# First batch's rows loaded and normalised ahead of the context, and two exponentials moved by one product

## The chip, the cores and the metric

The kernel runs on one core of one Trainium2 chip. The metric is the device time of one execution in microseconds (us). A core has five engines, each with its own instruction queue: PE (TensorE, matrix products), DVE (VectorE, elementwise work and reductions), ACT (ScalarE, functions and copies), POOL (GpSimd, elementwise work beside DVE) and SP (SyncE, which issues most of the loads and stores). ACT can issue loads too. Engines wait for each other through semaphores.

## The reference, cut to what matters

Two decoder layers over x, of two batches, 512 rows of 1024 columns each, with a context of 1024 rows of 1024 columns per batch. All is float32.

```python
x = x + L0_xattn(layernorm(x), ctx)   # fake_quant(x1) @ fake_quant(ctx)
x = x + L0_ffn(layernorm(x))          # linear, plus a mixture of low-rank terms
x = x + L1_xattn(layernorm(x), ctx, ctx, mask)   # 32 heads, 8 key/value heads, rotary
x = x + L1_ffn(layernorm(x))          # linear, plus one low-rank expert per row

def layernorm(x):
    return (x - mean(x)) / sqrt(var(x) + 1e-5)
def fake_quant(x, s, z):
    return (clip(round(x / s + z), 0, 255) - z) * s
```

Layer 0's attention is a plain product of the quantized, normalised rows with the quantized context. Layer 1's keys and values depend on the context alone, so they need nothing of layer 0.

## The kernel before, in words

**Products.** Large float32 products go block by block through a form with seven block products in place of eight (`seven`, `seven_onto`). The seven products need sums and differences of the input blocks (`left_steps`, L233 to L241, for the weights; `right_steps`, L247 to L255, for the context), and the results are put together again by additions on DVE (L278, L281, L283, L287, L290). The products stand on PE in the order 1, 2, 6, 7, 5, 4, 3, and each adds up in a PSUM bank; there are four such banks (tag `b`), so a product can also wait for DVE or ACT to have read an older bank. One product is four matrix multiplications of 128 by 512, shown in the profile as eight matmuls (L345), about 3.43 us.

**The first stage.** The keys of the first batch come first, while the weights and the context arrive. `first` holds four chains of products: two heads of quad 0 (`first[0]`) and two of quad 1 (`first[1]`). Their products 1 and 2 use raw blocks and need nothing of DVE. Product 6 of the first head is the first that needs DVE: L250 and L236. A finished key block is rotated (`rope_steps`, two ACT copies L204 and L205, then L207, L210 and L211 on DVE) and written away (`kT`, L487). This stage is written inside a block in which DVE and ACT keep the program's order; the PE order is as written in the whole kernel. All the other instructions are placed by a scheduler, which may also put later work between those of the block. So where an instruction stands on its engine is read from the built program, not from the source.

**Loads.** SP issues the weights, the context and the rotary tables, then a list of small constants: the four quantization scales and zero points (L1066), router and gate constants (L1067 to L1070). The rows of the first batch (`load_rows(0, nc.scalar)`) are issued by ACT, behind the first stage.

**Layer 0 beside the keys.** `layer_0` is a chain of side steps. `weave` advances it by one step after every second product of the main work, which is the rest of `first[1]` (ten products), then the values, and so on. For a batch, `quantized_product` loads eight context row blocks, quantizes each in three DVE operations (L182, L185, L186) into `q2`, then takes four row blocks: statistics (two L151 and one L152), square root on ACT (L163), reciprocal (L164), scaling (L156), quantizing (L182, L185, L186). Two steps behind, `turned` transposes a row block on PE (L424), copies it out and forms its row sum on ACT (L427). Then come the column sums (L447) and the product (L461) with its additions.

**Start of attention.** The last queries' products are worked off in the first turns of `attention` (`extra["products"]`). For each head the scores (L763) go to two wide PSUM tiles and are added to the mask on DVE (L777); a tree of maxima follows (L785 to L791), which PE transposes (L727, also into a wide tile) and DVE reduces (L729). `place_maximum` copies the maximum to PSUM on ACT (L805), and `exponential(j)` adds it on DVE (L809) and takes the exponential on ACT (L812). In the turn before the first head is attended to, four query products are done, numbered by `i`; before, the first exponential follows product `i == 1` and the second `i == 2`.

Of the kernel before, what the change touches and what calls it, by code (L numbers as in the profile page):

```python
# [13 lines left out]
BF16 = mybir.dt.bfloat16  # L14
# [25 lines left out]
def decoder_kernel(  # L40
# [38 lines left out]
    def u8(shape, dtype=F32):  # L79
        return new(shape, "u8", 14, dtype)  # L80

    def u4(shape, dtype=F32):
        return new(shape, "u4", 17, dtype)
# [56 lines left out]
    def copy_out(dst, src):  # L140

        evac[0] += 1
        if evac[0] % 2:
            nc.scalar.copy(dst, src)
        else:
            nc.vector.tensor_copy(dst, src)
# [12 lines left out]
    def layernorm(x_t):  # L159
        mv = small([P, 2])  # L160
        moments(x_t, mv)
        rstd = small([P, 1])
        nc.scalar.activation(rstd, mv[:, 1:2], AF.Sqrt, bias=eps_t)  # L163
        nc.vector.reciprocal(rstd, rstd)  # L164
        return scaled(x_t, mv[:, 0:1], rstd)
# [14 lines left out]
    def quantized(dst, src, side):  # L180

        nc.vector.tensor_scalar(  # L182
            src, src, qp[f"{side}_inv"], qp[f"{side}_zp"], ALU.mult, ALU.add
        )
        nc.vector.tensor_scalar(src, src, 0.0, QMAX, ALU.max, ALU.min)  # L185
        nc.vector.tensor_scalar(dst, src, RND, RND + QMID, ALU.add, ALU.subtract)  # L186
# [185 lines left out]
    def rows(b, t):  # L372
        return x[b][t // 2][:, t % 2, :]
# [33 lines left out]
        return right_sums(nc.vector, *quarters, lambda: u8([P, 4, HALF]))  # L407


    def quantized_product(b):  # L410
        q2 = [u8([P, 4, D], BF16) for _ in range(2)]
        for k in range(NKT):
            c_t = u4([P, D])
            nc.sync.dma_start(c_t, ctx_in[b, ts(k, P), :])
            quantized(q2[k // 4][:, k % 4, :], c_t, "x2")
            if k % 2:
                yield
        x1T = u8([P, NC, S], BF16)
        rsum, l1s = [], []

        def turned(t):
            tr = ps_wide().bitcast(BF16)[:, 0 : NC * P].rearrange("p (c n) -> p c n", c=NC)
            for c in range(NC):
                nc.tensor.transpose(tr[:, c, :], l1s[t][:, ts(c, P)], ident_b)  # L424
            copy_out(x1T[:, :, ts(t, P)], tr)
            r = small([P, 1])
            nc.scalar.activation(u4([P, D]), l1s[t], AF.Copy, accum_out=r)  # L427
            nc.vector.tensor_scalar(r, r, c_x2, None, ALU.mult)
            rsum.append(r)

        for t in range(NT):
            h = layernorm(rows(b, t))
            l1 = u2([P, D], BF16)
            quantized(l1, h, "x1")
            l1s.append(l1)
            if t > 1:
                turned(t - 2)
            yield
        turned(NT - 2)
        yield  # L440
        turned(NT - 1)


        cs = ps_wide()
        for n in range(2):
            for k in range(NKT):
                nc.tensor.matmul(  # L447
                    cs[:, ts(n, HALF)],
                    ones_b,
                    q2[k // 4][:, k % 4, ts(n, HALF)],  # L450
                    start=(k == 0),
                    stop=(k == NKT - 1),
                )
        csum = u4([P, D])
        nc.vector.tensor_scalar(csum, cs, kc2, c_x1, ALU.add, ALU.mult)
        yield
        for t in range(NT):
            acc = ps_wide()
            for n in range(2):
                for c in range(NC):  # L460
                    nc.tensor.matmul(  # L461
                        acc[:, ts(n, HALF)],
                        x1T[:, c, ts(t, P)],
                        q2[c // 4][:, c % 4, ts(n, HALF)],
                        start=(c == 0),
                        stop=(c == NC - 1),
                    )
            y = u4([P, D])
            nc.vector.scalar_tensor_tensor(y, acc, rsum[t], csum, ALU.add, ALU.add)
            xs = rows(b, t)  # L470
            nc.vector.scalar_tensor_tensor(xs, y, s12, xs, ALU.mult, ALU.add)
            yield
# [378 lines left out]
    def attention(extra):  # L851

        total = B * NH
        heads, outs, kv = {}, {}, {}
        stretches = iter(())

        def rotate():  # L860
            for rotation in extra["later"]:
                next(rotation, None)
            extra["later"].clear()

        def begin(n):
            if n >= total:
                return
            gg = n // GRP
            if gg not in kv:
                b, g = gg // NKV, gg % NKV  # L870
                kT = u4([P, S2])
                nc.sync.dma_start(kT, kT_d[b][g])
                v = u4([P, NKT, DH])
                nc.sync.dma_start(v, v_d[b][g // 2][:, :, ts(g % 2, DH)])
                kv[gg] = kT, v
                outs[gg] = u8([P, GRP, S])
            heads[n] = Head(n, kv[gg], outs[gg][:, n % GRP, :])

        begin(0)
        for n in range(-2, total + GRP + 1):  # L880
            new, mid, old = heads.get(n + 2), heads.get(n + 1), heads.get(n)
            begin(n + 3)
            if new:
                for j in range(4):
                    new.scores(j)
            yield

            if n - 1 in heads:
                heads.pop(n - 1).normalize()
            if n == GRP - 1 or n == NH:  # L890
                fetch_rows(n // NH)

            if GRP <= n <= total and n % GRP == 0:
                oT = outs.pop(n // GRP - 1)
                sums = u8([P, 3, 2, 256])
                places = iter(range(3))
                o_ops = left_sums(
                    nc.gpsimd,
                    oT[:, 0:2, 0:256],
                    oT[:, 2:4, 0:256],  # L900
                    oT[:, 0:2, 256:S],
                    oT[:, 2:4, 256:S],
                    lambda: sums[:, next(places)],
                )
                following = n // GRP - 1, o_ops
            tree = new.tree() if new else iter(())
            k = (n - 1) % GRP
            if n > GRP and k == 0:
                gg, o_ops = following
                stretches = projection(gg // NKV, o_ops, dict(w_ops))  # L910
            for _ in range(3 + k % 2 if n > GRP else 0):
                next(stretches, None)
                next(tree, None)
            if n > GRP and gg + 1 < B * NKV:
                for i in {2: (1, 6, 2), 3: (7, 5, 4, 3)}.get(k, ()):
                    w_ops[i] = output_operand((gg + 1) % NKV, i)
            for i in range(extra.pop(n, 0)):
                for _ in range(2):
                    next(tree, None)
                next(extra["products"])  # L920

                if mid and not old and i == 1:
                    mid.place_maximum()
                    mid.exponential(0)
                if mid and not old and i == 2:
                    mid.exponential(1)
            if n == GRP:
                w_ops = {i: output_operand(0, i) for i in (1, 6, 2, 7, 5, 4, 3)}
            for _ in tree:
                pass  # L930
            yield

            if mid and old:
                mid.place_maximum()
            if old:
                old.turn_sum()
            elif new:
                new.turn_maximum()
            rotate()
            if old:  # L940
                old.attend(0)
                if mid:
                    mid.exponential(0)
                if new:
                    new.turn_maximum()
                if mid:
                    mid.exponential(1)
                old.den = from_row(old.den)
            if new:
                new.nmx = from_row(new.nmx)  # L950
            if old:
                old.attend(1)
            yield
# [114 lines left out]
    nc.sync.dma_start(eb_t, ebias.partition_broadcast(P))  # L1068
    nc.sync.dma_start(r0_t, r0T.rearrange("(c p) e -> p c e", p=P))
    nc.sync.dma_start(ga_t, gaT.rearrange("(c p) e -> p c e", p=P))  # L1070


    ctx_ops = [ctx_raw[0], ctx_raw[2]] + [None] * 5
# [5 lines left out]
    first = [keys(0, 0, ctx_ops, w[0], begun), keys(0, 1, ctx_ops, w[1])]  # L1079

    def layer_0():
        yield from quantized_product(0)
        put_away(0)
        x[1] = halves()
        load_rows(1, nc.sync)
        yield from quantized_product(1)

    with tc.manual_schedule(engines={mybir.EngineType.DVE, mybir.EngineType.Activation}):
# [25 lines left out]
        for i, _ in enumerate(chain(*first[0])):  # L1114
            if i in (4, 5, 6, 7):
                w[1][:] = next(lefts) or w[1]

        x[0] = halves()
        load_rows(0, nc.scalar)

    for side in ("x1", "x2"):
        nc.vector.reciprocal(qp[f"{side}_inv"], qp[f"{side}_scale"])
# [309 lines left out]
```

## Time and profile before

| what | us |
|---|---|
| median of 4 runs | 2437.22 |
| lowest and highest run | 2435.51 and 2437.6 |
| the profiled execution | 2435.51 |
| its span, first to last instruction | 2433.7 |
| PE busy | 2405.6 |
| DVE busy | 1841.5 |
| POOL busy | 1025.1 |
| ACT busy | 527.5 |

The granted clock of PE is 0.999 of full speed over the span. The page gives busy times by engine, a strip of the span in forty slices, the transfers, the chain of work that ended last and the costliest groups of instructions. A group's row names the source line, the engine, the operation, the tile written and those read, the shape, the count, then busy time, the mean of one in ns, and the idle time of the engine before them with what ended it. The waits' rows give the total, the number and the longest. Rows in order of time begin with the start and the length, and end with the idle time before them in brackets. Buffer numbers are left out of names.

### The profile page before, as it was taken

What the parts mean: (1) busy time and instruction counts of PE and PEld (TensorE: products, weight loads), DVE (VectorE), ACT (ScalarE), POOL (GpSimd) and SP (SyncE); (2) the same over time, 40 slices, a digit from 0 to 9 for tenths busy, and PEclk for the clock granted to TensorE, in tenths of its full rate; (3) what the DMA queues carried; (4) which work ended last, traced back from release to release, by engine and by line L of the source; (5) the groups of instructions that cost most, each with busy time, mean ns of one, the idle gap of its engine ahead of it and who ended that gap; (6) DMA issues with size and microseconds to landing.
All of it is one profiled execution on the core that took longest, in us unless ns stands there. A gap on an engine that the chain in (4) does not pass through costs nothing.

```text
span 2433.7 us, 19521 instructions
## 1 busy us (share of the span) xinstructions
PE 2405.6 (99%) x6784; PEld 1194.2 (49%) x6792; DVE 1841.5 (76%) x1998; ACT 527.5 (22%) x623; POOL 1025.1 (42%) x543
## 2 busy tenths in 40 slices
PE   9999999999999999999999999999999999999999
PEld 4477458654444444444444444444444444444444
DVE  5849774345886556898888888888898988888753
ACT  1210221011222222322222222222223222222210
POOL 0000010210000001777676767667776767677531
PEclk9999999999999999999999999999999999999999
DMA  5437233013796221344234423542442344233501
GB/s 197 169 102 278 70 134 109 26 61 116 271 331 223 78 87 55 95 149 116 68 86 108 117 66 91 143 140 76 135 117 78 92 126 116 67 91 109 173 9 61
DMA packets 151506, 288.01 MB, mean 118 GB/s; under 512 B 32112, under 2 KB 49776, under 8 KB 149104
## 3 DMA queue, kind: packets, MB, share of 16 engines
q1 hardware_dynamic: 110880, 244.54, 31.6%
q10 hardware_dynamic: 40384, 41.70, 5.9%
q8 instruction: 54, 0.88, 0.2%
q0 software_dynamic: 144, 0.52, 0.1%
q14 instruction: 44, 0.36, 0.1%
HBM read 223.54 MB, written 63.18 MB: 118 GB/s over the span
## 4 chain that ended last, share of the span: by engine, by line
PE 55%; DVE 4%; issue 1%; POOL 0%; ACT 0%; POOLq 0%; ACTq 0%; DVEq 0%
PE b L345 20%; PE wide L763 16%; PE b L826 16%; PE wide L727 2%; DVE u L809 1%; DVE u L789 0%; DVE u L787 0%; DVE small L729 0%; DVE u L777 0%; DVE u L318 0%; PE b L967 0%; PE wide L192 0%; DVE u L791 0%; POOL u L818 0%; POOL u L819 0%
## 5 line engine op out<-in xcount | busy, mean ns | idle before, releaser
L345 PE MATMUL b<-u,u 128*128 128x512 f32 (+1 forms) x3600 | 1383.4, 541 | 17.0 <-DVE u L283 5.5
L345 PEld LDWEIGHTS b<-u,u 128*128 128x128 f32 x3600 | 680.4, 190 | 686.0 <-issue 603.5
L826 PE MATMUL b<-u,u 128*128 128x512 f32 x1024 | 460.3, 593 | 0.0
L763 PE MATMUL wide<-u,u 128*128 128x512 f32 x1024 | 452.4, 593 | 2.5 <-DVE u L777 1.8
L815 POOL TENSOR_TENSOR u<-u 128x1024 f32<-128x1024 f32 x64 | 151.6, 2368 | 707.0 <-ACT u L812 698.4
L777 DVE TENSOR_TENSOR u<-wide,u 128x1024 f32<-128x1024 f32 x256 | 312.7, 1223 | 126.1 <-PE wide L763 125.8
L812 ACT ACTIVATE u<-u 128x2048 f32<-128x2048 f32 x128 | 244.7, 1911 | 655.7 <-DVE u L809 651.3
L763 PEld LDWEIGHTS wide<-u,u 128*128 128x128 f32 x1024 | 192.9, 190 | 250.7 <-issue 175.6
L809 DVE TENSOR_TENSOR u<-u,b 128x2048 f32<-128x2048 f32 x128 | 290.1, 2267 | 3.0 <-ACT b L805 3.0
L826 PEld LDWEIGHTS b<-u,u 128*128 128x128 f32 x1024 | 186.2, 192 | 184.6 <-issue 184.6
L300 POOL TENSOR_TENSOR u<-u,u 128x512 f32<-128x512 f32 x120 | 184.4, 1563 | 170.3 <-DVE u L312 134.6
L318 DVE TENSOR_TENSOR u<-u,b 128x512 f32<-128x512 f32 x200 | 135.7, 679 | 121.7 <-PE b L345 114.3
L818 POOL TENSOR_TENSOR u<-u,u 128x1024 f32<-128x1024 f32 x64 | 150.7, 2354 | 30.6 <-ACT u L812 30.2
L819 POOL TENSOR_TENSOR u<-u,u 128x1024 f32<-128x1024 f32 x64 | 150.7, 2355 | 5.0
L837 POOL TENSOR_TENSOR u<-u,u 128x512 f32<-128x512 f32 x64 | 116.8, 1826 | 18.9 <-DMA u<-row 18.8
L204 ACT ACTIVATE u<-u 64x512 f32<-64x512 f32 x72 | 45.2, 628 | 361.9 <-DVE u L283 166.3
L785 DVE TENSOR_TENSOR u<-u 128x1024 f32<-128x1024 f32 x64 | 111.6, 1744 | 0.0
L727 PEld LDWEIGHTS wide<-ident,u 128*128 128x128 f32 x512 | 80.0, 203 | 62.2 <-issue 56.2
L605 POOL TENSOR_TENSOR u<-u,u 128x1024 f32<-128x1024 f32 x8 | 20.2, 2529 | 213.1 <-DVE u L156 210.5
L787 DVE TENSOR_TENSOR u<-u,u 128x1024 f32<-128x1024 f32 x64 | 106.5, 1664 | 0.2
L820 POOL TENSOR_TENSOR u<-u 128x512 f32<-128x512 f32 x64 | 100.1, 1563 | 5.0
L1158 POOL DMA_DIRECT2D u<-in_b_dram x1 | 0.7, 717 | 228.4 <-PE b L345 228.4
(136 smaller groups left out, 1638.5 us busy)
## 6 DMA issues: line engine op xcount, KB each, us to landing
u<-row ACTq DMA_DIRECT2D x128, 256.0 KB, 3.7
u<-wo SPq DMA_DIRECT2D x64, 512.0 KB, 4.6
u<-in_wo_dram SPq DMA_DIRECT2D x48, 512.0 KB, 4.6
u<-in_wq_dram SPq DMA_DIRECT2D x32, 512.0 KB, 4.3
q<-u SPq DMA_DIRECT2D x64, 256.0 KB, 2.3
u<-in_wo_dram SPq DMA_DIRECT2D x16, 1024.0 KB, 7.7
wo<-u SPq DMA_DIRECT2D x32, 512.0 KB, 3.5
u<-q SPq DMA_DIRECT2D x64, 256.0 KB, 4.5
```

Source lines behind the costliest of these rows:

```text
L300: nc.gpsimd.tensor_tensor(c, c, what, ALU.add)
L318: nc.vector.tensor_tensor(c, c, acc, ALU.add)
L345: nc.tensor.matmul(acc, lhsT, rhs, start=start and k == 0, stop=k == len(pairs) - 1, skip_group_check=True,)
L727: nc.tensor.transpose(tr[:, t, :], src[:, t, :], ident)
L763: nc.tensor.matmul(sc[:, ts(n, HALF)], self.kT[:, ts(2 * j + n, P)], self.qT, start=True, stop=True,)
L777: nc.vector.tensor_tensor(self.e[j // 2][:, js, :], sc.rearrange("p (k q) -> p k q", k=2), mask[j], ALU.add)
L809: nc.vector.tensor_tensor(e, e, self.nmf.unsqueeze(1).to_broadcast([P, 4, S]), ALU.add)
L812: nc.scalar.activation(e, e, AF.Exp)
L815: nc.gpsimd.tensor_tensor(d, e[:, 0:2, :], e[:, 2:4, :], ALU.add)
L818: nc.gpsimd.tensor_tensor(d, d, e[:, 0:2, :], ALU.add)
L819: nc.gpsimd.tensor_tensor(d, d, e[:, 2:4, :], ALU.add)
L826: nc.tensor.matmul(self.acc, self.v[:, k, :], self.e[j][:, k % 4, :], start=(k == 0), stop=(k == NKT - 1),)
```

## The change

The rows of batch 0 are issued by SP, directly behind the constants, instead of by ACT behind the first stage. For batch 0 alone `quantized_product` takes the rows ahead of the context. There the statistics of all four row blocks come first, one square root and one reciprocal serve all four, and then each block is scaled and quantized as before. The order for batch 1 stays: context, then rows, a root for each. In `attention` both exponentials of the first head are called one product later.

```diff
-    def quantized_product(b):
-        q2 = [u8([P, 4, D], BF16) for _ in range(2)]
-        for k in range(NKT):
-            c_t = u4([P, D])
-            nc.sync.dma_start(c_t, ctx_in[b, ts(k, P), :])
-            quantized(q2[k // 4][:, k % 4, :], c_t, "x2")
-            if k % 2:
-                yield
-        x1T = u8([P, NC, S], BF16)
-        rsum, l1s = [], []
+    def quantized_product(b, rows_first=False):
+        q2, x1T, rsum, l1s = [], [], [], []
+
+        def quantized_context():
+            q2.extend(u8([P, 4, D], BF16) for _ in range(2))
+            for k in range(NKT):
+                c_t = u4([P, D])
+                nc.sync.dma_start(c_t, ctx_in[b, ts(k, P), :])
+                quantized(q2[k // 4][:, k % 4, :], c_t, "x2")
+                if k % 2:
+                    yield
...
-        for t in range(NT):
-            h = layernorm(rows(b, t))
-            l1 = u2([P, D], BF16)
-            quantized(l1, h, "x1")
-            l1s.append(l1)
-            if t > 1:
-                turned(t - 2)
-            yield
-        turned(NT - 2)
-        yield
-        turned(NT - 1)
+        def quantized_rows():
+            x1T.append(u8([P, NC, S], BF16))
+            mv, rstd = small([P, NT, 2]), small([P, NT])
+            if rows_first:
+                for t in range(NT):
+                    moments(rows(b, t), mv[:, t, :])
+                nc.scalar.activation(rstd, mv[:, :, 1], AF.Sqrt, bias=eps_t)
+                nc.vector.reciprocal(rstd, rstd)
+            for t in range(NT):
+                if rows_first:
+                    h = scaled(rows(b, t), mv[:, t, 0:1], rstd[:, t : t + 1])
+                else:
+                    h = layernorm(rows(b, t))
+                l1 = u2([P, D], BF16)
+                quantized(l1, h, "x1")
+                l1s.append(l1)
+                if t > 1:
+                    turned(t - 2)
+                yield
+            turned(NT - 2)
+            yield
+            turned(NT - 1)
+
+        parts = [quantized_context, quantized_rows]
+        for part in reversed(parts) if rows_first else parts:
+            yield from part()
...
                 if mid and not old and i == 1:
                     mid.place_maximum()
-                    mid.exponential(0)
-                if mid and not old and i == 2:
-                    mid.exponential(1)
+                if mid and not old and i > 1:
+                    mid.exponential(i - 2)
...
     nc.sync.dma_start(ga_t, gaT.rearrange("(c p) e -> p c e", p=P))
+    x[0] = halves()
+    load_rows(0, nc.sync)
...
     def layer_0():
-        yield from quantized_product(0)
+        yield from quantized_product(0, True)
...
-        x[0] = halves()
-        load_rows(0, nc.scalar)
```

More of the change, by code (lines that the diff above doesn't have):

```diff
@@ L424, in turned @@
                 nc.tensor.transpose(tr[:, c, :], l1s[t][:, ts(c, P)], ident_b)
-            copy_out(x1T[:, :, ts(t, P)], tr)
+            copy_out(x1T[0][:, :, ts(t, P)], tr)
             r = small([P, 1])
@@ L462, in quantized_product @@
                         acc[:, ts(n, HALF)],
-                        x1T[:, c, ts(t, P)],
+                        x1T[0][:, c, ts(t, P)],
                         q2[c // 4][:, c % 4, ts(n, HALF)],
```

## The prediction

> **What bounds the kernel now.** I read the page's busy shares first, then the waits of PE (TensorE), then the time-ordered rows of DVE (VectorE) where those waits lie.
>
> ```profile
> PE 2405.6 (99%) x6784; PEld 1194.2 (49%) x6792; DVE 1841.5 (76%) x1998; ACT 527.5 (22%) x623; POOL 1025.1 (42%) x543
> ...
> L345 PE MATMUL b<-u,u 128*128 128x512 f32 (+1 forms) x3600 | 1383.4, 541 | 17.0 <-DVE u L283 5.5
> ```
>
> PE is busy for 2405.6 of 2433.7 us, so an edit pays only by the PE idle time that it removes or makes. In the first 400 us the waits of PE are:
>
> ```profile
> PE b L345 <- DVE u L283: 4.2, 2, 3.4
> PE b L345 <- ACT u L274: 4.1, 1, 4.1
> PE b L345 <- DVE u L281: 3.9, 3, 1.6
> ```
>
> Behind the first stand these DVE rows (start, length, idle before in brackets):
>
> ```profile
> 77.79 0.69 DVE L151 BATCH_NORM_STATS2 small<-u 128x6 f32<-128x512 f32 x1 [2.39 <-DMA u<-in_x_in_dram]
> ...
> 84.78 0.81 DVE L182 TENSOR_SCALAR u<-u,qp_x_inv,qp_x_zp 128x1024 f32<-128x1024 f32 x1 [1.74 <-DMA u<-in_ctx_in_dram]
> 85.51 0.68 DVE L283 TENSOR_TENSOR u<-u,b 128x512 f32<-128x512 f32 x1
> ```
>
> DVE works in order: while L182 waits for a context row, L283, which PE needs, stands behind it, and PE idles 82.83 to 86.25. The ACT wait of 4.12 (121.92 to 126.04) is the same on the scalar engine: copy L274 stands behind square root L163, which waits for a row's statistics. Between lie waits of 1.27 and 0.75; together 9.56. Two stretches also ran at half clock (length, busy, ..., PEclk, DMA):
>
> ```profile
> 85.80:89.20 3.40, 2.95 (x4) 1.40 (x5) 3.40 (x6) 1.26 (x2) 0.00 (x0) 0.50 1.03 413
> 126.75:130.17 3.42, 3.42 (x9) 2.68 (x9) 3.28 (x6) 0.77 (x2) 0.00 (x0) 0.50 1.04 375
> ```
>
> Half of the PE time in them is lost: (89.21 - 86.25)/2 = 1.48 and 3.42/2 = 1.71, so 3.2. What the stage after 45 us loses is 9.56 + 3.2 = 12.8.
>
> **Part 1, what is saved.** Rows go first: their statistics, one root and four scalings are done before the context rows are wanted, and quantizing the context (eight rows of 0.72 + 0.60 + 0.60 = 1.93 by L182, L185, L186, 15.4 in all) moves into the first value products, where DVE owes PE one 0.6 operation per 3.43 us product. So all four waits can go. The new order still has four rows' scaling and quantizing, 4 x (0.72 + 1.93) = 10.6, in the key products; one late L281 there may leave about 0.6 (estimate; ends 0, and 3.4 as the longest such wait before). Saved: 12.8 - 0.6 = 12.2. The four row loads leave ACT's queue (0.33 to 0.46 each), which is not the bound; on SP they stand ahead of the first kT write, which nobody waits for in this stage. The context loads now stand behind kT writes on SP; before they landed 4.0 to 10.6 us after issue. Quantizing starts with the value products, near 118 (111 before, plus some 7 that Part 2 costs by then beyond what is saved), takes 15.4, and shares DVE with the last key rotations (some 6): done near 140. The column sums of L447, which need all eight rows, are due near 150, so the cover is some 10 us.
>
> **Part 2, what it costs.** The built order of the changed kernel shows what the diff does not. On DVE the six small operations on the quantization constants (L1122 to L1126 before) now stand ahead of the first difference L247, and a BN_STATS of row 0 stands between L247 and L250. Before:
>
> ```profile
> 20.13 2.29 DVE L247 TENSOR_TENSOR u<-u,u 128x2048 f32<-128x2048 f32 x1 [18.20 <-DMA u<-in_ctxT_in_dram]
> 24.10 2.29 DVE L250 TENSOR_TENSOR u<-u,u 128x2048 f32<-128x2048 f32 x1 [1.68 <-DMA u<-in_ctxT_in_dram]
> 26.31 1.22 DVE L233 TENSOR_TENSOR u<-u,u 128x1024 f32<-128x1024 f32 x1
> 27.56 1.22 DVE L236 TENSOR_TENSOR u<-u,u 128x1024 f32<-128x1024 f32 x1
> 28.70 0.68 DVE L207 SCALAR_TENSOR_TENSOR u<-b,cos_t 128x512 f32<-128x512 f32 x1
> ```
>
> The constants' loads are issued at 17.3 to 24.0 and land 10.8 to 4.6 us later, all near 28.1 to 28.6. So L247 starts at 29.1 instead of 20.13. Steps from start to start: 2.20 for 2048 columns, 1.14 for 1024, 0.60 for 512 or a BN_STATS, 0.12 for an aggregate. L247 ends its step at 31.3. Row 0 is issued behind the last constant (27.97 + 0.4 = 28.4). A load of the same 512 KB on a quiet SP queue (in_wv) took 4.0 to 4.8; I take 4.0, so 32.4. Below it is ga_t's 2.7 (144 KB, the load just ahead), above it 5.7, the first x row before, which shared the queues with context loads. Then:
> - BN 0.6, L250 2.2, L233 1.14, BN 0.6, L236 1.14, L207 0.68 to its end: 38.8. Product 6 of the first head needs them and the PSUM bank that L207 frees; PE comes to it at 12.56 + 6 x 3.43 = 33.1. PE waits 5.7.
> - L207, L210, aggregate, BN, L211, L252, L238, L207 to its end: 38.1 + 0.6 + 0.6 + 0.1 + 0.6 + 0.6 + 2.2 + 1.1 + 0.7 = 44.7, product 7. It runs to 48.1.
> - L210, BN, L211, L241, L255, aggregate, three BN, aggregate, L207 from 44.5: 0.6 + 0.6 + 0.6 + 1.1 + 2.2 + 0.1 + 1.8 + 0.1 + 0.7 = 52.4: product 5 waits 4.3 for the next bank.
> - L210, BN, L211, aggregate, L207, L210 to 55.4; reciprocal behind the one root on ACT (table load 1.28 + 0.30 after the aggregate at 54.3, 55.9; behind the root on ACT stands L204, which waits for L283 until 58.8 anyway); L211, L278 with its 0.78 step, L281 to its end: 58.1, product 4.
>
> Product 4 started at 44.74 before (after a wait of 0.94): 13.4 later. DVE sets this time all along, so PE's clock in it hardly counts. Part 1 and 2: 13.4 - 12.2 = +1.2.
>
> The trace went to half clock after the waits of 3.42 and 4.12, for 3.41 us each, from 85.79 and 126.75; in the 3.41 us before these points PE had still worked 0.45 and 0.71 us. The Trainium skill (TensorE: Matmul & The Clock Gate, Part 1) has a free-running window of about 3.4 us and a drop after at least one idle window. By its letter neither wait here should have brought the drop, and of the new ones only the 5.7 one must. The sum is the same by both: with a full clock product 5 would end 1.4 earlier and product 4 still wait for L281 until 58.1.
>
> The same page (Architectural detail) calls ACT and DVE strict FIFO. This rule speaks against the change, and the rows at 77.79 to 85.51 bear it out. Were it not so, L247 could pass the waiting constants, and the time would be that of the first rival below.
>
> **Part 3, exponentials a product later.** Before (PE, then DVE, at the start of attention):
>
> ```profile
> 959.29 3.70 PE L345 MATMUL b<-u,u 128*128 128x512 f32 x8 [1.25 <-DVE u L278]
> ```
>
> ```profile
> 956.35 2.29 DVE L809 TENSOR_TENSOR u<-u,b 128x2048 f32<-128x2048 f32 x1 [2.98 <-ACT b L805]
> 958.56 0.68 DVE L278 TENSOR_TENSOR u<-u,b 128x512 f32<-128x512 f32 x1
> 959.15 2.28 DVE L809 TENSOR_TENSOR u<-u,b 128x2048 f32<-128x2048 f32 x1
> 963.03 0.69 DVE L281 TENSOR_TENSOR u<-u,b 128x512 f32<-128x512 f32 x1 [1.60 <-PE b L345]
> 963.64 0.68 DVE L729 TENSOR_REDUCE small<-wide 128x4 f32<-128x512 f32 x1
> ```
>
> In the new order L278 comes before the first L809 and L281 before the second. L278 then starts when its product ends, 958.08 instead of 958.56: saved 0.5. But the second L809 (2.20) now stands between L281 (962.55) and the reduction L729: 962.55 + 0.6 + 2.2 = 965.35, ending at 966.05. L729 frees the PSUM tile of the second score pair of L763, which PE wants at 962.8 + 1.7 = 964.5: a new wait of 1.5. The third pair wants the tile that the first L777 frees at 965.35 + 3 x 0.6 + 1.2 = 968.4, and PE is there at 967.85: 0.55, and some 0.1 for restarting. Net +1.7. The rest of the shift is covered: the second exponential on ACT (L812, 1.91, begun at 961.47 before) ends near 967.5 instead of 963.4, and its first reader, attend (L826), starts at 977.6; the row of the next maximum is issued on ACT behind it (L736, 964.35 before), 3 us later, lands near 973 and is copied by L805 at 981. Ends: -1.25 if both new waits are covered, +2.2 if the old wait stays.
>
> **Sum.** +1.2 + 1.7 = +2.9. The profiled execution took 2435.5 (span 2433.7 and 1.8 around it), the lowest of the four runs; the median is 2437.2, so the times would be 2438.4 and 2440.1. I say 2440.
>
> **Rivals.**
> - Faster: the constants land early enough not to hold DVE. For it: they are 0.5 KB each. Against: landings of 4.6 to 10.8 us behind the weights. Without the 9 us the stage costs eight BN_STATS and four aggregates (5.3) instead of 13.4, total -5.2: 2432. It decides if L247 starts by about 21. Chance 0.08.
> - Slower: row 0 lands late, as the x rows did before (5.7, 8.1, 9.6, 11.2). Each us past 4.0 moves product 4 by one us; past 6.0 the whole is over 0.2% slower. At 8.1: +7.0, 2444. For it: the rows follow ten loads on one queue. Against: the queues are nearly empty at 28 us. Chance 0.24.
> - DVE stays short in the key products, since it also carries 10.6 us of row work; waits like the old 3.42 return. Price +3 to +4: 2443. Against: no row waits for a load there. Chance 0.16.
>
> **How the numbers follow.** The forecast has 0.52. Its own ends are -1.3 and +1.7 (row 0), +-1.5 (where the clock's steps fall) and -3.0 to +0.5 (part 3), roughly 2436 to 2443. Leaving out the faster rival and half of the slow one gives 2434.5 to 2445. Within 0.2% (4.9 us, about what a measurement of this kernel can tell from no change) lie most of the forecast and half of the third rival: 0.54. Slower: 0.39. Faster: 0.07.
>
> **What would show it.** DVE idle until about 28.6, then L247, then about 1 us waiting for in_x; PE waits on L345 of some 5.7 and 4.3 between 33 and 53; none over 1 from 60 to 150; L763 waiting for L729 near 964. It is wrong if L247 still starts near 20, if row 0 lands beyond 6 us, or if waits of 2 us or more remain in the key products.

## Result and the profile after

The changed kernel takes 2441.12 us (median of 35 runs, 2438.0 to 2444.0) where the kernel before takes 2437.55 (median of 55). The ratio is 1.0015, with a 95% interval of 1.0011 to 1.0020: 3.6 us slower, and clearly so, though by less than 0.2%. Forecast were 2440.0 and +2.9. The profiled execution took 2442.7 (span 2440.9), 7.2 more than the profiled one of before; the pair of profiles exaggerates the change, for a reason that comes below.

PE stays the bound. The page's first part and its largest group, of the changed kernel:

```profile
PE 2408.7 (99%) x6784; PEld 1194.3 (49%) x6792; DVE 1839.7 (75%) x1995; ACT 527.3 (22%) x620; POOL 1025.5 (42%) x543
...
L345 PE MATMUL b<-u,u 128*128 128x512 f32 (+1 forms) x3600 | 1386.1, 542 | 18.6 <-DVE u L207 9.4
```

The matmuls of L345 are idle ahead for 18.6 us instead of 17.0, and the main releaser is another one: the rotation L207 (keys), no longer the sums L281 and L283. The waits of PE in the first 400 us (total, times, longest) say where:

```profile
PE b L345 <- DVE u L207: 9.4, 2, 5.8
PE b L345 <- DVE u L281: 2.3, 2, 1.7
```

The waits of 3.42, 1.27, 0.75 and 4.12 us in the kernel before are gone, and two of 5.78 and 3.65 have come. DVE's rows, in order of time, show how they come about:

```profile
28.00 0.16 DVE L1136 RECIPROCAL qp_x_inv<-qp_x_scale 128x1 f32<-128x1 f32 x1 [26.08 <-DMA qp_x_scale<-in_x_scale_dram]
...
28.77 2.28 DVE L247 TENSOR_TENSOR u<-u,u 128x2048 f32<-128x2048 f32 x1
32.95 0.69 DVE L151 BATCH_NORM_STATS2 small<-u 128x6 f32<-128x512 f32 x1 [1.90 <-DMA u<-in_x_in_dram]
33.56 2.27 DVE L250 TENSOR_TENSOR u<-u,u 128x2048 f32<-128x2048 f32 x1
...
59.32 0.69 DVE L283 TENSOR_TENSOR u<-u,b 128x512 f32<-128x512 f32 x1 [0.81 <-PE b L345]
```

DVE stands idle for 26.08 us, until a constant of 0.5 KB lands at 28; L247, which ran at 20.13 before, starts at 28.77; then DVE waits 1.90 us for row 0 before it may start L250 (24.10 before). L283 runs at 59.32, against 44.79 before. What PE made of it, in its own rows (start, length, instructions, and the idle time before):

```profile
39.35 9.81 PE L345 MATMUL b<-u,u 128*128 128x512 f32 x16 [5.78 <-DVE u L207]
52.81 9.47 PE L345 MATMUL b<-u,u 128*128 128x512 f32 x15 [3.65 <-DVE u L207]
...
344.64 5.85 PE L345 MATMUL b<-u,u 128*128 128x512 f32 x13 [1.70 <-DVE u L281]
...
963.21 3.70 PE L345 MATMUL b<-u,u 128*128 128x512 f32 x8 [0.85 <-DVE u L278]
...
970.49 1.98 PE L779 MATMUL wide<-u,u 128*128 128x512 f32 x4 [1.39 <-DVE small L745]
972.82 3.70 PE L779 MATMUL wide<-u,u 128*128 128x512 f32 x8 [0.34 <-DVE u L793]
...
995.28 3.70 PE L779 MATMUL wide<-u,u 128*128 128x512 f32 x8 [0.65 <-DVE u L793]
```

(Lines of attention stand 16 lower than before: scores L763 are now L779, the reduction L729 is L745, the additions of the mask L777 are L793.) The wait for L278 is 0.85 instead of 1.25, and three new waits follow, for the reduction and twice for an addition of the mask behind it.

The row at 344.64 is a useful mark. The same product, with much the same wait ahead of it, stands in the profile before:

```profile
343.18 7.13 PE L345 MATMUL b<-u,u 128*128 128x512 f32 x16 [1.65 <-DVE u L281]
```

Everything that parts 1 and 2 of the change touch lies ahead of it, part 3 far behind it. So it splits one profile into three stretches: to this mark (parts 1 and 2), from it to the product that waits for L278 near 959 (no part of the change), and from there to the transposes that wait for L791 (L807 after) near 1043 (part 3). The table below has all runs of this study, the differences of medians taken against the kernel before in the same series, the stretches from each kernel's one profile:

| kernel | against before, us | 95% interval of the ratio | mark near 343, against 343.18 | mark to L278's product | from there to L791's transposes |
|---|---|---|---|---|---|
| before | | | 0 | 616.1 | 84.1 |
| changed | +3.6 | 1.0011 to 1.0020 | +1.5 | 618.6 | 86.8 |
| exponentials undone | +1.2 | 0.9997 to 1.0015 | +2.1 | 617.1 | 83.6 |
| exponentials alone | +2.6 | 1.0005 to 1.0022 | +0.4 | 615.9 | 86.8 |
| constants early | +4.0 | 1.0007 to 1.0025 | +3.2 | 614.7 | 86.8 |
| rows by hand | +1.6 | 0.9996 to 1.0014 | +1.2 | 612.8 | 86.8 |
| rows and constants by hand | -3.5 | 0.9974 to 0.9991 | -6.7 | 618.4 | 86.8 |
| statistics between, exponentials undone | -11.1 | 0.9937 to 0.9962 | -12.3 | 618.4 | 83.6 |
| statistics between | -8.1 | 0.9945 to 0.9972 | -12.5 | 621.6 | 86.8 |
| rows late | +4.7 | 1.0006 to 1.0024 | +1.3 | 615.9 | 86.8 |

The middle stretch runs from 612.8 to 621.6 us though no kernel changes anything in it: in all ten profiles each engine's instructions, from 2 us behind the mark to 6 us ahead of L278's product, are the same and in the same order. It is as long as its waits make it. PE's waits of more than 0.25 us there add up to 1.36 us in the shortest and 8.42 in the longest; waits of up to 2 us between 600 and 760 come and go (one of 2.04 at 664.70 in the changed kernel's profile). That is how two single profiles can be 7.2 us apart where the medians are 3.6 apart. What makes these waits come and go stays open, and it need not be chance alone: constants early and rows by hand, which have the shortest middle stretches, are by their medians 1.9 and 2.3 us faster than their other two stretches add up to, and the two kernels with the statistics between 1.7 slower. So a median prices an edit only to some 2 us, and the stretch that holds the edit is the better measure.

### The profile page after: what moved, and what is told of

Its sections match the earlier page's. It is cut to its first block, busy times and chain, and to the rows that moved or that the text cites. A ratio compares the mean times of both kernels' runs of the same rounds, so it can differ in the third digit from the quotient of the medians.

```text
span 2440.9 us, 19522 instructions
## 1 busy us (share of the span) xinstructions
PE 2408.7 (99%) x6784; PEld 1194.3 (49%) x6792; DVE 1839.7 (75%) x1995; ACT 527.3 (22%) x620; POOL 1025.5 (42%) x543
## 4 chain that ended last, share of the span: by engine, by line
PE 84%; DVE 9%; DMA 3%; issue 2%; POOL 1%; ACT 1%; SPq 0%; POOLq 0%; DVEq 0%; ACTq 0%
PE b L345 47%; PE wide L779 16%; PE b L842 15%; PE wide L743 2%; DVE u L825 2%; DMA u<-in_wo_dram 1%; PE wide L477 1%; PE wide L192 1%; DMA u<-in_wk_dram 1%; DVE u L207 1%; DVE u L210 1%; PE b L667 1%; DVE small L745 0%; DVE u L805 0%; DVE u L793 0%
## 5 line engine op out<-in xcount | busy, mean ns | idle before, releaser
L345 PE MATMUL b<-u,u 128*128 128x512 f32 (+1 forms) x3600 | 1386.1, 542 | 18.6 <-DVE u L207 9.4
L345 PEld LDWEIGHTS b<-u,u 128*128 128x128 f32 x3600 | 680.8, 191 | 688.1 <-issue 605.6
L779 PE MATMUL wide<-u,u 128*128 128x512 f32 x1024 | 453.3, 594 | 5.0 <-DVE u L793 2.5
L793 DVE TENSOR_TENSOR u<-wide,u 128x1024 f32<-128x1024 f32 x256 | 312.6, 1223 | 126.0 <-PE wide L779 125.8
L828 ACT ACTIVATE u<-u 128x2048 f32<-128x2048 f32 x128 | 244.7, 1912 | 661.1 <-DVE u L825 647.8
L779 PEld LDWEIGHTS wide<-u,u 128*128 128x128 f32 x1024 | 192.7, 190 | 254.2 <-issue 177.2
L834 POOL TENSOR_TENSOR u<-u,u 128x1024 f32<-128x1024 f32 x64 | 150.7, 2354 | 32.4 <-ACT u L828 32.2
L204 ACT ACTIVATE u<-u 64x512 f32<-64x512 f32 x72 | 45.2, 628 | 340.4 <-DVE u L283 152.8
```

What stands on the lines that cost most here:

```text
L345: nc.tensor.matmul(acc, lhsT, rhs, start=start and k == 0, stop=k == len(pairs) - 1, skip_group_check=True,)
L779: nc.tensor.matmul(sc[:, ts(n, HALF)], self.kT[:, ts(2 * j + n, P)], self.qT, start=True, stop=True,)
L793: nc.vector.tensor_tensor(self.e[j // 2][:, js, :], sc.rearrange("p (k q) -> p k q", k=2), mask[j], ALU.add)
L828: nc.scalar.activation(e, e, AF.Exp)
L834: nc.gpsimd.tensor_tensor(d, d, e[:, 0:2, :], ALU.add)
```

## Experiments

**The exponentials undone.** The changed kernel with part 3 taken back:

```diff
                 if mid and not old and i == 1:
                     mid.place_maximum()
-                if mid and not old and i > 1:
-                    mid.exponential(i - 2)
+                    mid.exponential(0)
+                if mid and not old and i == 2:
+                    mid.exponential(1)
```

> The changed kernel with the exponentials put back to their old products (part 3 undone). By the sum of the prediction part 3 costs 1.7 us, so this kernel is 1.7 faster than the changed one: about +1.9 against before where the changed kernel has +3.6. The waits on L345 of 5.8 and 3.7 us between 33 and 53 us stay, and at the start of attention only the old wait of 1.25 us for L278 is left; the reduction and the first shifted copy hold up no score product. Rival: part 3 costs nothing, since waits merely changed places; then +3.6 stays, and parts 1 and 2 cost all of it.

Measured +1.2 against before, 2.4 less than the changed kernel. The first stage's waits are in place (5.82 and 3.95), and product 4 starts at 59.70, where it started at 44.74 before. At the start of attention PE's rows have only the old wait:

```profile
962.30 3.70 PE L345 MATMUL b<-u,u 128*128 128x512 f32 x8 [1.26 <-DVE u L278]
```

The rival, in which part 3 costs nothing, falls: without it the third stretch is back at 83.6.

**The exponentials alone.** The kernel before with the same edit the other way round.

> The kernel before with only the exponentials moved (part 3 alone). Theory: +1.7 us against before (ends -1.25 and +2.2); PE waits for the reduction of the first maximum some 1.4 us and for the copy behind it some 0.4 us near 960, and 0.85 instead of 1.25 for L278; the first 900 us are as before. Rival: no change within 0.5 us.

Measured +2.6. The waits of PE from 950 to 1000 us:

```profile
PE wide L763 <- DVE small L729: 1.4, 1, 1.4
PE wide L763 <- DVE u L777: 1.0, 2, 0.7
```

The two expected waits are there, with 1.39 and 0.34, and a third of 0.66 that was not expected: the slip reaches the next batch of score pairs, 25 us later (how, is said in the next section). In all seven kernels with part 3 the stretch from 959 takes 86.8 us, in the three without it 83.6 to 84.1. That is 2.7 to 3.2, less the 0.4 gained ahead of L278: part 3 costs 2.3 to 2.8 us.

**The constants early.** The four small loads move from the end of SP's list to ACT, right behind its context loads; DVE keeps its order.

```diff
     load_context(nc.sync, 1, 0, slice(2, 4))
+    for name, ap in qparams.items():
+        nc.scalar.dma_start(qp[name], ap.partition_broadcast(P))
...
-    for name, ap in qparams.items():
-        nc.sync.dma_start(qp[name], ap.partition_broadcast(P))
```

> The changed kernel with the four loads of the quantization constants issued by ACT behind its context loads, not by SP behind all weights; the order of DVE is the same. Theory: L247 starts near 20 instead of 28.8, but row 0 still lands near 33, its BN_STATS still stands ahead of L250, and L250 still starts near 33.6: PE waits 5.8 and 3.7 as before, and the time is that of the changed kernel (+3.6) within 1 us. Rival, as the prediction's faster rival has it: the constants are what holds DVE, and without their wait the stage costs 5.3 instead of 13.4 or more, so the kernel is some 8 us faster than the changed one, -5 against before.

Measured +4.0: no gain. DVE's rows:

```profile
23.39 2.29 DVE L247 TENSOR_TENSOR u<-u,u 128x2048 f32<-128x2048 f32 x1 [6.47 <-DMA u<-in_ctxT_in_dram]
34.49 0.69 DVE L151 BATCH_NORM_STATS2 small<-u 128x6 f32<-128x512 f32 x1 [8.80 <-DMA u<-in_x_in_dram]
35.10 2.27 DVE L250 TENSOR_TENSOR u<-u,u 128x2048 f32<-128x2048 f32 x1
```

The constants are done at 17, L247 no longer waits for them, and DVE then stands 8.80 us for row 0 instead. PE waits 6.26 and 3.41. The mark is later than in the changed kernel (+3.2 against +1.5) because row 0, issued at 28.1 (28.25 there), took 6.4 us to land instead of 4.7 (why, no run shows): L250 starts 1.5 later, and product 6 with it (40.89 against 39.35). PE also has a new wait of 1.76 us for a context load at 8.5, but it costs nothing, since PE reaches product 6 at 34.6 and stands there until 40.89. So the constants' wait costs nothing as long as the row's wait stands behind it.

**The rows by hand.** The constants stay in front of L247, and the four rows' statistics are put one row ahead of each of four steps in the hand-written first stage (`all_moments`, which is already in the kernel, gives a row's two BN_STATS and aggregate at each step, then the root, then the reciprocal).

```diff
+        stats = all_moments(0)
         for i, _ in enumerate(chain(*first[0])):
+            if i in (0, 1, 2, 3, 8, 9):
+                ready = next(stats)
             if i in (4, 5, 6, 7):
                 w[1][:] = next(lefts) or w[1]
...
-        yield from quantized_product(0, True)
+        yield from quantized_product(0, ready)
```

> The changed kernel with the four rows' statistics placed by hand between the products of the first stage (from product 6 on), and the constants' operations still ahead of L247. Theory, in which both waits count: L247 starts at 28.8 as in the changed kernel, L250 at 31.0 instead of 33.6; L233, L236 and L207 end at 36.2, so PE waits 3.0 instead of 5.8 for product 6, then some 1.7 twice; product 4 starts near 51 instead of 59.3. The statistics, 5.3 us, then still have to be done, so the gain against the changed kernel is 8.3 - 5.3 = 3.0 us: about +0.6 against before. Rival: only the row's wait counts; then product 6 waits less than 1 us and the time is about -5 against before. Other rival: only the constants count; then +3.6 stays.

Measured +1.6, and the waits lie as worked out: 3.37 for product 6, then 1.56. But the statistics now stand between L278 and L281 and between L281 and L283, in the path that frees PE's banks, and PE pays three times, 2.14 here and then 2.13 and 2.32 near 71 and 90:

```profile
36.77 8.96 PE L345 MATMUL b<-u,u 128*128 128x512 f32 x16 [3.37 <-DVE u L207]
...
53.13 17.43 PE L345 MATMUL b<-u,u 128*128 128x512 f32 x40 [2.14 <-DVE u L281]
```

**Rows and constants by hand.** The same, and the constants' operations go behind L255 and its rotations:

```diff
             for g in first[1]:
                 next(g)
+        for side in ("x1", "x2"):
+            nc.vector.reciprocal(qp[f"{side}_inv"], qp[f"{side}_scale"])
...
         lefts = left_steps(nc.vector, *wk_raw[1], lambda: u4([P, 4, 256]))
```

> The changed kernel with both waits taken out of the front of DVE's first stage: the six operations on the constants stand behind L255 and its rotations, and the four rows' statistics go one row ahead of each of the steps from product 7 on. Theory (both waits together hold product 4): L247 starts near 20, product 6 has no wait, product 4 starts near 45 as in the kernel before; the statistics, 5.3 us, sit between the sums of the first stage and cost PE two or three waits of 2 to 2.5 us. Sum: 12.2 saved, 7 for these waits, 1.7 for the exponentials: -3.5 against before, ends -6 and -2. Rival, the row's wait alone: the same time as with the statistics alone placed by hand, +1.6. Other rival, the early row loads hold up the loads of the first stage: a wait for a load remains before 35 us.

Measured -3.5. Product 6 waits for nothing; waits of 1.64, 2.12 and 1.35 for L281 are left. With the last kernels this is a square of four, read where product 4 of the first head starts: 59.1 in the changed kernel, 60.9 without the constants' wait (1.5 of the difference is row 0's later landing), 53.1 without the row's wait, 46.2 without both. The constants' wait alone is worth nothing, because the row's wait behind it ends later; once that is gone, it is worth 6.9. (At the mark the third has lost its lead, +1.2 against +1.5 in the changed kernel, since the rows' new place costs PE the waits for L281.)

**The statistics in DVE's gaps.** In the kernel before, DVE is idle 1.33 us ahead of each rotation L207 of the first stage, while ACT copies the two halves (L204, L205). One row's statistics are 1.3 us. In the last version (rows and constants by hand) they go there, and the exponentials go back; the lines are against that version:

```diff
+    between = [iter(())]
+
     def rope(dst, acc, half, scale):
 
         for _ in rope_steps(dst, acc, half, scale, nc.vector):
-            pass
+            next(between[0], None)
...
         stats = all_moments(0)
+        between[0] = islice(stats, NT)
         for i, _ in enumerate(chain(*first[0])):
-            if i in (0, 1, 2, 3, 8, 9):
+            if i in (7, 8):
                 ready = next(stats)
```

> As the version with the statistics by hand, but each row's two BN_STATS and aggregate (1.3 us) stand where DVE waits for the two rotations on ACT (L204, L205: 1.33 us idle each time in the kernel before), and the exponentials stand in their old places. Theory: the statistics then cost PE nothing; 12.2 saved, none of it given back, some 0.6 left in the key products: -11.5 against before, ends -13 and -8, no wait of PE over 1 us between 35 and 160 us and a full clock throughout. Rival: the row work in the key products (10.6 us of scaling and quantizing) runs DVE short whatever the first stage does; then waits of 2 us or more come back between 60 and 130, and the gain is under 5.

Measured -11.1 (2425.5 us): this version beats both kernels by 11 and 15 us. DVE's rows (lines from L200 on are two lower here, so L285 is L283 of before and L209 is L207):

```profile
45.40 0.69 DVE L285 TENSOR_TENSOR u<-u,b 128x512 f32<-128x512 f32 x1
46.01 1.28 DVE L151 BATCH_NORM_STATS2 small<-u 128x6 f32<-128x512 f32 x2
...
47.45 0.67 DVE L209 SCALAR_TENSOR_TENSOR u<-u,u 128x512 f32<-128x512 f32 x1
```

The rotation starts 2.05 us behind L285; before, it started 2.02 behind L283 with nothing between them (44.79 and 46.81). The row costs 0.03. The stretch from 34 to 160 us (length; PE, PEld, DVE, ACT, POOL busy; granted clock; DMA) shows PE busy for all but 1.3 us, at full clock:

```profile
34.00:160.00 126.00, 124.69 (x438) 75.26 (x440) 97.08 (x153) 26.81 (x42) 0.00 (x0) 1.00 0.35 120
```

The kernel before had 115.45 and a clock of 0.97 in this stretch, the changed one 116.38 and 0.95. The rival, that DVE runs short in the key products whatever the first stage does, falls: between 46 and 329 us the longest wait is 0.63.

**The statistics in DVE's gaps, exponentials as in the change.** The same kernel with part 3 left in.

> The version with the statistics in DVE's waits for ACT, with the exponentials a product later as in the changed kernel. Theory: some 1.7 us slower than the version with the exponentials in their old places (-10 against before), with the waits of 0.85, 1.39 and 0.34 us at the start of attention. Rival: the two are the same within 0.5 us.

Measured -8.1, so part 3 costs 3.0 here, more than the 1.7 expected, with waits of 0.85, 1.39, 0.34 and 0.67.

**The rows late.** The changed kernel with `load_rows(0, nc.scalar)` back behind the first stage; rows ahead of the context and the one root stay.

```diff
-    x[0] = halves()
-    load_rows(0, nc.sync)
...
                 w[1][:] = next(lefts) or w[1]
 
+        x[0] = halves()
+        load_rows(0, nc.scalar)
```

> The changed kernel with the rows loaded as before, by ACT behind the first stage; rows ahead of the context, the one root for all and the late exponentials stay. Theory: the first stage is that of the kernel before (L247 near 20, product 4 near 45). The rows, issued at 72 to 74 with no context loads beside them, land 4.7 to 6.9 later, to 80.8; DVE takes all four rows' statistics in one piece, then root, reciprocal, two scalings and the start of their quantizing stand ahead of L281, which ends near 89.3, while PE wants its bank near 79.4: one wait of some 10 us and 1.7 to 3.4 us of half clock behind it, against 12.8 saved, and 1.7 for the exponentials: +1.3 to +3 against before. Rival: with rows ahead of the context the waits are gone even with late rows; then -10.

Measured +4.7, outside what was expected, by the expected mechanism. The rows landed 5.7 to 8.8 us after issue rather than 4.7 to 6.9, and the one wait is 11.91, up to the end of this row of DVE:

```profile
90.78 0.68 DVE L281 TENSOR_TENSOR u<-u,b 128x512 f32<-128x512 f32 x1
```

L281, which frees PE's bank, stands behind all four rows' statistics, the root and the first quantizing. The half clock lasts from 83.18 to 96.83; PE works 5.31 us in it and loses half, 2.7. One root for all rows puts all of this in one piece ahead of L281, with a wait of 1.70 for the root in it; with rows that land this late that costs PE 11.91 us.

## Why the prediction was right, and where its steps were off

The forecast of +2.9 met +3.6 by the mechanism it named: what the key products gain, the first stage gives back. Point by point:

- **Saved, 12.2.** Product 4 started 14.4 us later in the changed kernel's profile (59.1 against 44.74), the mark near 343 only 1.5 later: 12.9 saved. In the version with the statistics in the gaps and the exponentials undone product 4 starts 0.6 late and the mark is 12.3 early: 12.9 again. The 0.6 left for a late L281 came as 0.57. The missing 0.7 is a price of waiting that the sum did not have. A row of 8 matmuls lasts 3.70 us, one of 16 lasts 7.13: 3.43 for each product, and 0.27 once for each uninterrupted row. So a wait costs about 0.27 more than its idle column says; three waits fewer give 0.8. The Trainium skill (TensorE: Matmul & The Clock Gate, Step-by-step: what each phase is for) says that in a stream the drain of one matmul overlaps the fill of the next, and that one standing alone can't hide its drain. The rows here agree in kind; which part of the 0.27 is drain no run here shows.
- **The first stage, 13.4.** It was 14.4. L247 at 28.77 (29.1 predicted), row 0 landing at 32.9, 4.7 us after its issue (32.4 and 4.0), waits of 5.78 and 3.65 (5.7 and 4.3), product 5 at 52.81 (52.4): the built order, read as DVE's queue, gave the stage to half a microsecond up to here. The step that failed is "DVE sets this time all along, so PE's clock in it hardly counts". At the end it counts:

```profile
37.95:44.78 6.83, 5.42 (x7) 2.33 (x8) 6.83 (x9) 1.18 (x2) 0.00 (x0) 0.50 0.11 41
44.78:51.60 6.82, 4.38 (x11) 1.63 (x9) 6.82 (x10) 0.00 (x0) 0.00 (x0) 1.00 0.10 38
51.60:58.43 6.83, 5.62 (x7) 2.52 (x8) 6.18 (x13) 1.58 (x2) 0.00 (x0) 0.50 0.17 64
```

  These stretches of the changed kernel show the clock at half (0.50) twice, for 6.83 us each, not for 3.41 as in the kernel before. Product 5 therefore ran until 59.3, its end overlapping the start of product 4 at 59.1; L281 was done at 58.5, and it was DVE's L283 that waited 0.81 us for PE, not product 4 for L281 at 58.1. Of the missing 1.0, 0.4 is DVE's and 0.6 the clock's. In the kernel with the exponentials undone the second half clock lasted only 3.41 us, and there product 4 did wait for L281 (0.36).
- **Part 3, +1.7 with ends of -1.25 and +2.2.** It is +2.3 to +2.8, above the upper end. The saving (0.4 for 0.5) and the first two waits (1.39 for 1.5, 0.34 for 0.55) were right. What was missed: 0.25 to 0.27 for each of three waits, where the sum put 0.1 for all; and a third wait of 0.65 at the next score pairs. "The rest of the shift is covered" is the step that failed: it followed the second exponential to attend and to the next maximum, but not to POOL. These are rows of the changed kernel:

```profile
971.93 2.35 POOL L834 TENSOR_TENSOR u<-u,u 128x1024 f32<-128x1024 f32 x1 [2.19 <-ACT u L828]
...
986.38 0.69 DVE L287 TENSOR_TENSOR u<-u,b 128x512 f32<-128x512 f32 x1 [1.15 <-POOL u L211]
```

  POOL waits for the late exponential (L828, L812 before), the rotation's L210 and L211 stand behind its additions there, and DVE's L287 waits for that L211. This wait of 1.15 or 1.16 stands in all seven kernels with part 3 and in none of the three without.
- **Errors that cancelled.** The first stage was priced 1.0 too low and the saving 0.7 too low; part 3 was 0.6 to 1.1 too low. By the stretches the whole comes to 1.5 + 2.3 to 2.8, about 4, against 3.6 between the medians. That the sum for parts 1 and 2 was off by only 0.3 is luck in so far as two errors of opposite sign met.
- **The faster rival was priced wrongly.** It said that with early constants the total would be -5.2. The kernel with early constants is +4.0: L247 starts at 23.39 there, and row 0's landing at 34.5 holds L250 anyway. The rival needed both waits gone, and even then (-3.5) the place of the statistics mattered; in DVE's gaps they cost nothing, which the price of 5.3 for the eight BN_STATS and four aggregates did not see.
- **The slower rival** did not come true (row 0 took 4.7 us, not 8.1; in the six other kernels that load it early, 4.4 to 6.4), nor did **DVE short in the key products**: from 60 to 150 us the changed kernel's longest wait is 0.57, and the context's quantizing in the value products cost nothing up to the mark, as said.

## What to carry to other kernels

When an early load lets a scheduler move work forward, read the order on the in-order engine before believing in the gain: one small operation on a late constant, or one statistic of a late row, holds everything behind it, and of the two such waits here the earlier was hidden by the later, so that removing it alone showed nothing. Work of the right size was free in a gap that the engine has anyway (1.3 us of statistics in 1.33 us of waiting for ACT) and costly among the sums that free PE's banks: between these two places lie 4.6 us (-8.1 against -3.5). A mark, the same product in both profiles behind the part that was edited, tells a few microseconds apart that two whole spans do not.

## What the runs showed of the hardware

- **Half clock comes sooner and goes later than the prediction had it.** The granted clock changes in steps of 3.41 us. Between 20 and 2390 us of all ten profiles, each full-clock window in which PE was busy for 38% or less (fourteen of them) was followed by half clock, and each with 44% or more by full clock. One wait of 2.12 us was enough, as the windows of the kernel with rows and constants by hand show:

```profile
63.42:66.83 3.41, 1.29 (x4) 0.64 (x4) 3.41 (x5) 0.00 (x0) 0.00 (x0) 1.00 0.60 190
66.83:70.25 3.42, 3.42 (x6) 1.35 (x5) 1.99 (x4) 1.25 (x2) 0.00 (x0) 0.50 0.00 0
```

  And a half-clock window in which PE was busy for only 56% to 79% (six of them) was followed by another one; 87% to 100% brought full clock back. The Trainium skill (TensorE: Matmul & The Clock Gate, Why this matters for your kernels) warns of idle gaps over some 3 us; here 2.1 us sufficed when they fell inside one window, and the measurement decides.
- **A wait of PE costs about 0.27 us more than the idle time that the profile shows** (above). It shows at the start of attention too: waits of 0.85, 1.39, 0.34 and 0.65, less the old 1.25, are 2.0 us of idle time, and the stretches differ by 2.3 to 2.8.
